# A two-layer per-position convolution: x handed over in two further layouts, the output in the residual's layout, residuals and bias loaded nearer to their use, and one half of a third of the weight tiles evicted by ScalarE

## The chip, the core and the metric

One core of one Trainium2 chip runs the program. The metric is the device time of one execution in microseconds (us). The engines are PE (TensorE, matmul), DVE (VectorE), ACT (ScalarE), POOL (GpSimd) and SP (SyncE, which here only issues DMAs).

## What is computed

Two layers of the same form, on x of shape 32 x 32 x 64 x 256 (s, b, channel, position l), float32. Each layer adds to x a convolution of width 3 along l whose weights are different at every b and l, made by a small network from z. Cut to what matters:

```python
h = relu(layernorm(z @ W1 + b1))                   # z: (b, l, 16), h: (b, l, 128)
w = (h @ W2 + b2).reshape(B, L, CI, CO, K)         # 64 x 64 x 3 weights at every (b, l)
bias = (relu(layernorm(z @ Wb1 + bb1)) @ Wb2 + bb2).transpose(0, 2, 1)
xn = groupnorm(x)                                  # mean, variance over (b, channel, 8 positions), for each s
out = einsum('sbilk,bliok->sbol', unfold(xn), w) + bias[None]
x = x + out                                        # and the same again with the second layer's weights
```

The group norm takes its mean over all b, so layer 2 cannot begin before the last of layer 1 is done.

## The kernel before, in words

**Stage 1, `first_stats` (L230).** All of x (64 MB) is read once in 16 loads of 4 MB, three buffers round, for the statistics: 512 `bn_stats` on VectorE (L278), a `merge` (L299) after every second load. Between them, in `slot` (L254), the 32 steps of the hidden network run over all engines; hidden values and bias go to DRAM (`hd`, `bd`).

**The main loop (L535 on)** has 128 chunks v = 2u + h: u counts the 32 values of b in both layers (64), h the two halves of the 64 output channels. A chunk has two phases on PE.

- *Make*: 12 tiles `pg` of 16 matmuls each (`make`, L419; L426 and L427), three PSUM buffers round. A tile holds the weights of 8 output channels at 128 pairs of positions, and is of one of three kinds. `take` (L430) evicts it, adds b2, and scatters it into the one buffer `wall` (L439). Kinds 0 and 1 take one VectorE operation over 128 partitions; kind 2 goes to two places in `wall` and takes two of 64 partitions. The order of the tiles is the list `order` (L534): the four of kind 2 first, then eight of kinds 0 and 1.
- *Products* (`products`, L445): 160 matmuls (L456; 320 records in the trace) multiply `xn` by `wall` into four tiles `pc` (two buffers). VectorE adds each into the residual `ys` (L465); in layer 1 two `bn_stats` follow (L468) for layer 2's statistics.

The products of chunk v stand behind the first make tile of chunk v+1. After them `after(v)` (L506) queues the rest: `store` (L401, four DMAs on ACT's queue), `normalize` (L412, two POOL operations, L416) for half of the s of a later u, `load_pairs` (L121) of the next input of `normalize`, `load_residual(v+3)` (L129) into the buffer that the store has just left, `add_bias(v+3)` on POOL (L399), and `load_bias(v+4)` (L386). All loads are on SP's queue. Instructions and DMA issues of one engine run in the order written; POOL runs `normalize` for one chunk behind `add_bias` of the one before, so what the add waits for holds the normalization up as well.

**Layouts.** `load_pairs` reads [s, channel, l] in runs of 1 KB and twice over (the second time shifted by one position), of which `normalize` uses every other element. `load_residual` and `store` move [s, 32 channels, 64 positions] in runs of 256 bytes, 1 MB a chunk. At the change of layer `next_stats` (L339) turns the 512 results into mean and 1/deviation; its matmuls (L367) stand in PE's queue.

Of the kernel before, what the change touches and what calls it, by code (L numbers as in the profile page):

```python
# [30 lines left out]
P = 128  # L31
# [10 lines left out]
def conv_layers(ctx: ExitStack, tc: tile.TileContext, x: bass.AP, layers: list, out: bass.AP):  # L42
    nc = tc.nc
    S, B, C, L = x.shape
# [3 lines left out]
    M = L // 2  # L48
# [9 lines left out]
    SH = S // 2  # L58
    SPLIT = 2
    NS = S // SPLIT  # L60
# [22 lines left out]
    xt = room[:, 0 : SH * L].rearrange("p (s l) -> p s l", l=L)  # L83
# [4 lines left out]
    between = const.tile([P, GT, B, NH, 6], FP, name="between")  # L88
# [29 lines left out]
    def source(u):  # L118
        return x[:, u] if u < B else x1[u - B]

    def load_pairs(u, k):  # L121
        src = source(u)[k * SH : (k + 1) * SH].rearrange("s c l -> c s l")
        nc.sync.dma_start(out=xt[0:C], in_=src)
        nc.sync.dma_start(out=xt[C:P, :, 0 : L - 1], in_=src[:, :, 1:L])

    def residual(v):
        return ys[:, v % RING]

    def load_residual(v):  # L129
        u, h = divmod(v, NH)  # L130
        for t in range(NT):
            nc.sync.dma_start(  # L132
                out=residual(v)[t * S : (t + 1) * S],
                in_=source(u)[:, h * CH : (h + 1) * CH, t * LT : (t + 1) * LT],
            )
# [94 lines left out]
    def first_stats():  # L230


        NJ = 2
        with tc.tile_pool(name="stage", bufs=1) as stage:
            spare = stage.tile([P, C // 2 * L], FP, name="spare")
            flat = [xn.rearrange("p b m s -> p (b m s)"), room, spare]
            xs = [r[:, 0 : C // 2 * L].rearrange("p (c l) -> p c l", l=L) for r in flat]
            src = x.rearrange("(q s) b (h c) l -> q (s b h) c l", s=SPLIT, h=2)
            NX = len(xs)
            for q in range(NX):  # L240
                nc.sync.dma_start(out=xs[q], in_=src[q])
                if q == 0:
                    small = [small_weights(stage, par, n) for n, par in enumerate(layers)]
            half = stage.tile([P, SPLIT, P], FP, name="half")
            nc.vector.memset(half, 0.0)
            for h in range(SPLIT):
                nc.vector.memset(half[h * C : (h + 1) * C, h, :], 1.0 / C)
# [7 lines left out]
            def slot(s, work):  # L255

                if s in made:
                    made[s].project()
                if s - 2 in made:
                    made.pop(s - 2).bias()  # L260
                if s in made:
                    made[s].root()
                for k, f in enumerate(work):
                    if k == 6 and s - 1 in made:
                        made[s - 1].scale()
                    f()
                if not work and s - 1 in made:
                    made[s - 1].scale()
                if s + 1 < U // 2:
                    made[s + 1] = Hidden(stage, zts, small, s + 1)  # L270

            parts = None
            for q in range(NS):
                if q % NJ == 0:
                    parts = stage.tile([P, NJ, G, 6], FP, tag="parts", name="parts", bufs=2)

                def piece(g, parts=parts, q=q):
                    return lambda: nc.vector.bn_stats(  # L278
                        parts[:, q % NJ, g, :], xs[q % NX][:, :, g * E : (g + 1) * E]
                    )  # L280

                for s in range(2):
                    slot(2 * q + s, [piece(g) for g in range(s * G // 2, (s + 1) * G // 2)])
                if q + NX < NS:
                    nc.sync.dma_start(out=xs[q % NX], in_=src[q + NX])
                if q + NX == NS - 1:
                    for o0 in range(0, C, 2 * OG):
                        load_w2(0, o0, o0 + 2 * OG)
                if q == NS - 3:

                    load_pairs(0, 0)
                    for v in range(RING):
                        load_residual(v)
                if q % NJ == NJ - 1:
                    merge(stage, parts, q - NJ + 1, NJ, half)
            for s in range(2 * NS, 2 * NS + 2):
                slot(s, [])

    def merge(stage, parts, q0, nj, half):  # L299
        n = nj * G  # L300
        st = parts.rearrange("p j g (two f) -> p (j g) two f", two=2)
        count = C // 2 * E
        m = stage.tile([P, n], FP, tag="mm", name="mm")
        d = stage.tile([P, n], FP, tag="md", name="md")
        v = stage.tile([P, n], FP, tag="mv", name="mv")
        nc.vector.tensor_tensor(m, st[:, :, 0, 1], st[:, :, 1, 1], ALU.add)
        nc.vector.tensor_scalar(m, m, 0.5, None, ALU.mult)
        nc.vector.tensor_tensor(d, st[:, :, 0, 1], st[:, :, 1, 1], ALU.subtract)
        nc.vector.tensor_tensor(d, d, d, ALU.mult)
        nc.vector.tensor_tensor(v, st[:, :, 0, 2], st[:, :, 1, 2], ALU.add)  # L310
        nc.vector.scalar_tensor_tensor(v, d, count / 4.0, v, ALU.mult, ALU.add)
        pm = ps_g.tile([P, SPLIT, n], FP, tag="pg", name="pm")
        for h in range(SPLIT):
            nc.tensor.matmul(pm[:, h, :], half[:, h, :], m, start=True, stop=True)
        s0 = q0 * SPLIT
        to = "p g (j h) -> p h j g"
        fr = "p h (j g) -> p h j g"
        for h in range(SPLIT):
            r = slice(h * C, (h + 1) * C)
            nc.vector.tensor_tensor(d[r], m[r], pm[r, h, :], ALU.subtract)  # L320
        nc.scalar.copy(
            gmean[:, :, s0 : s0 + nj * SPLIT].rearrange(to, h=SPLIT), pm.rearrange(fr, g=G)
        )
        nc.vector.tensor_tensor(d, d, d, ALU.mult)
        nc.vector.scalar_tensor_tensor(v, v, 1.0 / count, d, ALU.mult, ALU.add)
        pv = ps_g.tile([P, SPLIT, n], FP, tag="pg", name="pv")
        for h in range(SPLIT):
            nc.tensor.matmul(pv[:, h, :], half[:, h, :], v, start=True, stop=True)
        r = stage.tile([P, SPLIT, n], FP, tag="mr", name="mr")
        nc.scalar.activation(r, pv, AF.Sqrt, bias=eps)  # L330
        for h in range(SPLIT):
            nc.vector.reciprocal(
                rstd[:, :, s0 : s0 + nj * SPLIT].rearrange(to, h=SPLIT)[:, h],
                r.rearrange(fr, g=G)[:, h],
            )

    def next_stats(prep):

        st = between.rearrange("p g b h (two f) -> p g (b h two) f", two=2)  # L339
        n = st.shape[2]  # L340
        shape = [P, GT, n]
        m = prep.tile([P, GT], FP, name="nm")
        nc.vector.tensor_reduce(m, st[:, :, :, 1], AX.X, ALU.add)
        nc.vector.tensor_scalar(m, m, 1.0 / n, None, ALU.mult)
        v = prep.tile([P, GT], FP, name="nv")
# [3 lines left out]
        d = prep.tile([P, GT], FP, name="nd")  # L349
# [20 lines left out]
    with tc.manual_schedule():  # L370
        hs = {}
        first_stats()

        wp = ctx.enter_context(tc.tile_pool(name="wall", bufs=1))
        bp = ctx.enter_context(tc.tile_pool(name="bias", bufs=1))
        prep = ctx.enter_context(tc.tile_pool(name="prep", bufs=1))
# [24 lines left out]
        def store(v):  # L401
            u, h = divmod(v, NH)
            to = x1[u] if u < B else out[:, u - B]
            for t in range(NT):
                nc.scalar.dma_start(
                    out=to[:, h * CH : (h + 1) * CH, t * LT : (t + 1) * LT],
                    in_=residual(v)[t * S : (t + 1) * S],
                )

        def normalize(u, k):  # L410
            ss = slice(k * SH, (k + 1) * SH)
            o = xn[:, u % 2, 1 : M + 1, ss].rearrange("p (g e) s -> p s g e", g=G)  # L412
            i = xt[:, :, 0:L:2].rearrange("p s (g e) -> p s g e", g=G)
# [16 lines left out]
        def take(pg, n, kind, o0):  # L430

            if kind < 2:
                parts = [(slice(0, P), CH + (1 + kind) * CH)]
            else:
                parts = [(slice(0, C), CH + F), (slice(C, P), 0)]
            for rows, a in parts:
                nr = rows.stop - rows.start
                a += o0 % CH
                nc.vector.tensor_tensor(  # L439
                    at(wall[rows, 0, a : a + 1], [[WT, NT], [F, MT], [1, OG]]),  # L440
                    pg[rows].rearrange("p o (t m) -> p t m o", t=NT),
                    b2[n][rows, kind, None, None, o0 : o0 + OG].to_broadcast([nr, NT, MT, OG]),
                    ALU.add,
                )

# [123 lines left out]
```

## Time and profile before

| what | value |
|---|---|
| median of 3 runs | 5458.36 us (5456.52 to 5467.07) |
| the profiled execution, its own time | 5456.63 us |
| its span, first to last instruction | 5454.8 us |
| mean granted TensorE clock | 0.909 |
| busy: PE / DVE / POOL / ACT | 79% / 60% / 37% / 2% |
| moved by DMA | 784.94 MB in 1,398,552 packets, 1,098,949 of them under 512 B |

The span is divided here into stage 1 (up to about 310 us, and the first chunk up to 365 us), 64 chunks of layer 1 (to 2867 us), the change of layer, and 64 chunks of layer 2. In rows of groups, "x" is the count, the two figures behind the first bar are total busy us and mean ns of one, behind the second bar stands the idle time of the engine before them, and after "<-" what ended most of it; "issue" is idle time in which the engine waited for no semaphore. In a timeline a row has start, length, engine, line, operation, tiles, count, and in brackets the idle time before it. In rows of waits the figures are total us, times, longest. PEld is the loading of weights into PE. In rows of stretches PEclk is the granted share of the clock, and the next figure the busy share of the 16 DMA engines.

### The profile page before, as it was taken

The numbers are of one execution on the slowest core, as the hardware profiler recorded it, in microseconds if no ns is written. First come the engines' busy times: TensorE is split into PE (matmuls) and PEld (weight loads), VectorE is DVE, ScalarE is ACT, GpSimd is POOL, SyncE is SP. The second block draws the span as 40 slices with busy tenths as digits, with TensorE's granted clock in tenths as the row PEclk, the third lists the DMA queues.
The fourth block names the chain that finished last, engine by engine and source line by source line (L and its number), as shares of the span: only waits on it lengthen the run. The fifth ranks groups of instructions, "written<-read, shape, count | busy, mean of one in ns | idle before, by whom it ended". The sixth has DMA issues, their size and how long they took to land.

```text
span 5454.8 us, 191315 instructions
## 1 busy us (share of the span) xinstructions
PE 4322.6 (79%) x90760; PEld 4033.9 (74%) x90760; DVE 3269.2 (60%) x3768; ACT 118.1 (2%) x181; POOL 2034.0 (37%) x618
## 2 busy tenths in 40 slices
PE   6878788788777787887777887787777777787787
PEld 4568777777777777777767777777777777777777
DVE  7866666566566666666656555555555555565555
ACT  3410000000000000000000000000000000000000
POOL 3453433433343343334324334334334334334332
PEclk7679999999999999999989988998988998999999
DMA  8886777777777787777777778778778777778775
GB/s 308 308 171 128 141 136 132 144 130 131 135 142 130 134 148 129 133 138 143 133 143 152 137 130 130 131 132 136 133 127 136 135 130 137 134 131 144 128 133 100
DMA packets 1398552, 784.94 MB, mean 144 GB/s; under 512 B 1098949, under 2 KB 1377545, under 8 KB 1378825
## 3 DMA queue, kind: packets, MB, share of 16 engines
q1 hardware_dynamic: 829960, 616.43, 59.8%
q10 hardware_dynamic: 567808, 156.28, 15.5%
q8 instruction: 711, 11.65, 1.0%
q14 instruction: 73, 0.59, 0.0%
HBM read 625.78 MB, written 146.80 MB: 142 GB/s over the span
## 4 chain that ended last, share of the span: by engine, by line
PE 41%; POOL 17%; DVE 16%; DMA 13%; issue 10%; SPq 2%; ACT 0%; POOLq 0%; ACTq 0%; DVEq 0%
PE pc L456 23%; DVE wall L439 13%; POOL xn L416 11%; PE pg L426 10%; PE pg L427 5%; POOL room L399 5%; DMA room<-x 5%; DMA room<-in_x_dram 4%; DMA out_dram<-room 2%; SPq L132 2%; DMA x<-room 2%; PE p L175 1%; DVE room L465 1%; DVE parts L278 1%; PE p L215 1%
## 5 line engine op out<-in xcount | busy, mean ns | idle before, releaser
L426 PE MATMUL pg<-hT,w2t 128*64 128x128 f32 x24576 | 2814.8, 274 | 249.6 <-DVE wall L439 200.3
L426 PEld LDWEIGHTS pg<-hT,w2t 128*64 128x64 f32 x24576 | 2682.6, 137 | 355.3 <-PE pg L427 263.8
L427 PE MATMUL pg<-hT,w2t 128*64 128x128 f32 x24576 | 2825.5, 275 | 29.7 <-issue 29.6
L439 DVE TENSOR_TENSOR wall<-pg,b 64x1024 f32<-64x1024 f32 (+1 forms) x2048 | 2480.1, 1221 | 413.8 <-PE pg L427 369.3
L427 PEld LDWEIGHTS pg<-hT,w2t 128*64 128x64 f32 x24576 | 2682.5, 137 | 32.3 <-issue 32.1
L456 PE MATMUL pc<-wall,xn 128*32 128x128 f32 (+2 forms) x40960 | 1261.8, 289 | 761.6 <-issue 424.6
L456 PEld LDWEIGHTS pc<-wall,xn 128*32 128x32 f32 x40960 | 1188.3, 129 | 843.5 <-issue 494.4
L399 POOL TENSOR_TENSOR room<-room,bt 128x2048 f32<-128x2048 f32 x128 | 581.5, 4543 | 3124.3 <-DMA room<-x 1415.1
L465 DVE TENSOR_TENSOR room<-pc,room 128x512 f32<-128x512 f32 x512 | 354.1, 692 | 1695.2 <-PE pc L456 1619.1
L416 POOL TENSOR_TENSOR xn<-xn,rstd 128x2048 f32<-128x2048 f32 x128 | 741.0, 5789 | 10.0
L416 POOL TENSOR_TENSOR xn<-room,gmean 128x2048 f32<-128x2048 f32 x128 | 598.2, 4674 | 42.3 <-DMA room<-x 14.7
L468 DVE BATCH_NORM_STATS2 between<-room 128x6 f32<-128x256 f32 x512 | 192.9, 418 | 8.7
L187 POOL TENSOR_TENSOR sq<-sq 128x512 f32<-128x512 f32 (+2 forms) x192 | 104.3, 543 | 180.1 <-ACT sq L179 167.6
L175 PE MATMUL p<-wc,zt 17*128 17x256 f32 x256 | 108.3, 593 | 33.4 <-DMA zt<-in_L_conv_z_dram 32.6
L175 PEld LDWEIGHTS p<-wc,zt 17*128 17x128 f32 x256 | 72.5, 297 | 56.9 <-issue 39.4
L202 PEld LDWEIGHTS p<-ident,hs 128*128 128x128 f32 x256 | 49.0, 219 | 54.1 <-issue 40.2
L215 PE MATMUL p<-ht,Wb 128*64 128x512 f32 x64 | 61.6, 1065 | 10.6 <-ACT ht L205 10.6
L202 PE MATMUL p<-ident,hs 128*128 128x128 f32 x256 | 60.6, 416 | 4.6 <-DVE hs L193 4.6
L278 DVE BATCH_NORM_STATS2 parts<-xn 128x6 f32<-128x256 f32 x192 | 64.0, 407 | 0.0
L353 ACT ACTIVATE nv<-nv,eps 128x8 f32<-128x8 f32 x1 | 0.3, 300 | 2571.8 <-DVE nv L352 2571.8
L278 DVE BATCH_NORM_STATS2 parts<-room 128x6 f32<-128x256 f32 x160 | 53.4, 409 | 0.0
L278 DVE BATCH_NORM_STATS2 parts<-spare 128x6 f32<-128x256 f32 x160 | 53.4, 408 | 0.0
(61 smaller groups left out, 271.3 us busy)
## 6 DMA issues: line engine op xcount, KB each, us to landing
bt<-bd SPq DMA_DIRECT2D x512, 256.0 KB, 5.0
room<-in_x_dram SPq DMA_DIRECT2D x64, 1024.0 KB, 9.0
room<-in_x_dram SPq DMA_DIRECT2D x256, 256.0 KB, 8.5
x<-room ACTq DMA_DIRECT2D x256, 256.0 KB, 5.3
room<-x SPq DMA_DIRECT2D x64, 1024.0 KB, 9.0
room<-x SPq DMA_DIRECT2D x256, 256.0 KB, 9.5
out_dram<-room ACTq DMA_DIRECT2D x256, 256.0 KB, 5.9
room<-in_x_dram SPq DMA_DIRECT2D x64, 1020.0 KB, 14.1
```

The source lines that it names most:

```text
L175: nc.tensor.matmul(self.p1[:, k], self.zt[:, k * P : (k + 1) * P], self.t["wc"], start=True, stop=True)
L202: nc.tensor.transpose(p2[:, net, k * P : (k + 1) * P], hs[:, 2 * k + net, :], ident)
L215: nc.tensor.matmul(p3, self.t["Wb2"], self.ht[:, 1, :], start=True, stop=True)
L278: return lambda: nc.vector.bn_stats(parts[:, q % NJ, g, :], xs[q % NX][:, :, g * E : (g + 1) * E])
L399: nc.gpsimd.tensor_tensor(y, y, bts.pop(v), ALU.add)
L416: nc.gpsimd.tensor_tensor(o, i, b, op)
L426: nc.tensor.matmul(pg[0:C, k, :], w[:, k0 * C : (k0 + 1) * C], h0, start=True, stop=True)
L427: nc.tensor.matmul(pg[C:P, k, :], w[:, k1 * C : (k1 + 1) * C], h1, start=True, stop=True)
L439: nc.vector.tensor_tensor(at(wall[rows, 0, a : a + 1], [[WT, NT], [F, MT], [1, OG]]), pg[rows].rearrange("p o (t m) -> p t m o", t=NT), b2 ...
L456: nc.tensor.matmul(pc[t * S : (t + 1) * S, n0 - q * EB : n1 - q * EB, :], xn[:, u % 2, t * MT + p + 1, :], wall[:, t, a : a + (n1 - n0) * CH],
L465: nc.vector.tensor_tensor(part, pc.rearrange("p n o -> p o n"), part, ALU.add)
L468: nc.vector.bn_stats(between[:, 2 * q + g, u, h, :], part[:, :, g * E : (g + 1) * E])
```

## The change

1. The host hands x over twice: `xs` in the residual's layout (partition = position block and s; a chunk is 8 KB in a row on each partition) and `xp` in the layout of pairs (partition = parity and channel, only the elements that `normalize` uses). In layer 1 `load_pairs` is one DMA of 1 MB and `load_residual` one DMA of 1 MB, both in runs of 8 KB. `xt` then holds both halves of a u, so `load_pairs` runs a whole u ahead. Layer 2 reads x1 as before. The output is stored in the layout of `xs`, one DMA a chunk.
2. Stage 1 reads `xs`; its `bn_stats` fill the same array that layer 2 uses, and one `stats` at the end takes the place of eight `merge`. The hidden steps are spread over the 512 `bn_stats` and end with them.
3. In `after(v)`: the store is on SP's queue, ahead of the loads; `load_residual(v+2)` goes into the buffer that chunk v-1 has left; `next_pairs` (normalize and load) comes before `add_bias(v+1)`, and `load_bias(v+2)` after it.
4. In `take`, kind 2: rows 0 to 63 by VectorE as before, rows 64 to 127 by eight ScalarE activations (Identity with a bias column), one for each output channel. The order of the tiles is 2, 0, 1 four times.

```diff
+        if u < B:
+            nc.sync.dma_start(out=t, in_=xp[u, k])
+        else:
+            src = x1[u - B][k * SH : (k + 1) * SH].rearrange("s c l -> c s l")
...
+            if kind < 2:
+                add(slice(0, P), CH + (1 + kind) * CH)
+            else:
+                add(slice(0, C), CH + F)
+                rows = slice(C, P)
+                for k in range(OG):
+                    nc.scalar.activation(
+                        place(rows, 0)[:, :, :, k],
+                        pg[rows, k].rearrange("p (t m) -> p t m", t=NT),
+                        AF.Identity,
+                        bias=b2[n][rows, kind, o0 + k : o0 + k + 1],
+                    )
...
+        def after(v):
+            u, h = divmod(v, NH)
+            if v >= 0:
+                store(v)
+            if v + 2 < NH * U:
+                load_residual(v + 2)
+            if v + 1 == NH * B:
+                stats()
+                for k in range(2):
+                    next_pairs(B, k)
+            w, k = (u + 1, 1) if h == 0 else (u + 2, 0)
+            if w != B:
+                next_pairs(w, k)
+            if v + 1 < NH * U:
+                add_bias(v + 1)
+            if v + 2 < NH * U:
+                load_bias(v + 2)
...
-        order = [(2, o) for o in starts] + [(kind, o) for o in starts for kind in range(2)]
+        order = [(kind, o) for o in starts for kind in (2, 0, 1)]
```

VectorE in a chunk of layer 1, before (b_0 is the bias b2 of layer 1, 64x4x32x8 a half tile, 128x4x32x8 a whole one):

```order
L465 TENSOR_TENSOR room<-pc,room 128x32x16
L468 BN_STATS between<-room 128x6 x2
L439 TENSOR_TENSOR wall<-pg,b_0_183 64x4x32x8 x8
L439 TENSOR_TENSOR wall<-pg,b_0_183 128x4x32x8 x8
L465 TENSOR_TENSOR room<-pc,room 128x32x16
```

and after the change:

```order
L442 TENSOR_TENSOR room<-pc,room 128x32x16
L445 BN_STATS parts<-room 128x6 x2
L401 TENSOR_TENSOR wall<-pg,b_0_184 64x4x32x8
L401 TENSOR_TENSOR wall<-pg,b_0_184 128x4x32x8 x2
L401 TENSOR_TENSOR wall<-pg,b_0_184 64x4x32x8
L401 TENSOR_TENSOR wall<-pg,b_0_184 128x4x32x8 x2
```

Sixteen evictions a chunk on VectorE have become twelve, and the half tiles stand one in three.

ScalarE after the change, the last half tile of one chunk, the load of the hidden values (hT) and the first half tile of the next chunk, with the semaphores that each row waits for (before, its queue in the loop held only DMA issues):

```order
L416 ACTIVATE wall<-pg,b_1_189 64x4x32 [waits DVE_49,Activation_49]
L416 ACTIVATE wall<-pg,b_1_189 64x4x32 [waits Activation_49] x7
L116 DMA hT<-hd_124 128x256 [waits DMAHW7_49,DMAHW1_49,PE_49]
L416 ACTIVATE wall<-pg,b_1_189 64x4x32 [waits DVE_49,PE_49,Activation_49]
L416 ACTIVATE wall<-pg,b_1_189 64x4x32 [waits Activation_49] x7
```

The first activation of a tile waits for a count of VectorE that stands for VectorE's half of the same tile; the first of a chunk waits for the products too, since they read `wall`. The counts of ScalarE itself are those of the chunk before.

SP's queue for one chunk of layer 2, before (x_12, x_13 are x1 of two values of b, L123 and L124 pairs, L132 residuals, L392 bias):

```order
L123 DMA room<-x_12_84 64x16x256
L124 DMA room<-x_12_84 64x16x255
L132 DMA room<-x_12_84 32x32x64 x4
L392 DMA bt<-bd_158 32x2048 x4
L123 DMA room<-x_13_85 64x16x256
```

and after (L372 is the store, L143 the residuals, L131 and L132 the pairs, L354 the bias):

```order
L372 DMA out_dram<-room 128x2048
L143 DMA room<-x_12_84 32x32x64 x4
L131 DMA room<-x_13_85 64x16x256
L132 DMA room<-x_13_85 64x16x255
L354 DMA bt<-bd_158 32x2048 x4
```

The store has come into SP's queue, one DMA in place of four on ACT's, and the residuals stand ahead of the pairs.

More of the change, by code (lines that the diff above doesn't have):

```diff
@@ L57, in conv_layers @@
     U = NL * B
[L58 to L60 removed]
+    SV = 4
     BLK = 2 * L
@@ L87, in conv_layers @@
     rstd = const.tile([P, G, S], FP, name="rstd")
-    between = const.tile([P, GT, B, NH, 6], FP, name="between")
+    parts = const.tile([P, GT, B, NH, 6], FP, name="parts")
+    prep = const.tile([P, 3, GT], FP, name="prep")
     ident = const.tile([P, P], FP, name="ident")
@@ L272, in first_stats @@
[L272 to L335, printed above, removed]
@@ L337, in next_stats, with step @@
-    def next_stats(prep):
-        st = between.rearrange("p g b h (two f) -> p g (b h two) f", two=2)
+            def step(s, half):
+                if half == 0:
+                    if s in made:
+                        made[s].project()
+                    if s - 2 in made:
+                        made.pop(s - 2).bias()
+                    if s in made:
+                        made[s].root()
+                else:
+                    if s - 1 in made:
+                        made[s - 1].scale()
+                    if s + 1 < U // 2:
+                        made[s + 1] = Hidden(stage, zts, small, s + 1)
```

198 lines of the change are left out of this document (106 added, 92 removed).

## The prediction, made before the changed kernel was run

> **What bounds the kernel now.** Read first are the spans of the page, its queues, and a row each from the rows of waits.
>
> ```profile
> span 5454.8 us, 191315 instructions
> PE 4322.6 (79%) x90760; PEld 4033.9 (74%) x90760; DVE 3269.2 (60%) x3768; ACT 118.1 (2%) x181; POOL 2034.0 (37%) x618
> q8 instruction: 711, 11.65, 1.0%
> q10 hardware_dynamic: 567808, 156.28, 15.5%
> POOL room L399 <- DMA room<-x: 1415.1, 58, 38.9
> PE pc L456 <- issue: 424.6, 204, 6.2
> PE pc L456 <- POOL xn L416: 335.2, 62, 8.2
> PE pg L426 <- DVE wall L439: 200.3, 406, 0.6
> ```
>
> PE is the engine to follow. It idles for three reasons, all in the main loop. For 424.6 us it waits for no semaphore in the products. For 335.2 us the products wait for POOL's normalization, which stands on POOL behind an add that waits for residuals (1415.1 us). For 200.3 us a make tile waits until VectorE has emptied a buffer.
>
> Next is the timeline of VectorE: the last products of a chunk (L465), from chunk to chunk.
>
> ```profile
> 365.43 0.69 DVE L465 TENSOR_TENSOR room<-pc,room 128x512 f32<-128x512 f32 x1 [0.58 <-PE pc L456]
> 1704.70 0.69 DVE L465 TENSOR_TENSOR room<-pc,room 128x512 f32<-128x512 f32 x1 [1.70 <-PE pc L456]
> 1706.10 13.42 DVE L439 TENSOR_TENSOR wall<-pg,b 64x1024 f32<-64x1024 f32 x11
> 1719.91 1.23 DVE L439 TENSOR_TENSOR wall<-pg,b 128x1024 f32<-128x1024 f32 x1 [0.38 <-PE pg L427]
> 1721.65 1.23 DVE L439 TENSOR_TENSOR wall<-pg,b 128x1024 f32<-128x1024 f32 x1 [0.52 <-PE pg L427]
> 1739.79 0.69 DVE L465 TENSOR_TENSOR room<-pc,room 128x512 f32<-128x512 f32 x1 [0.92 <-PE pc L456]
> 1782.93 0.69 DVE L465 TENSOR_TENSOR room<-pc,room 128x512 f32<-128x512 f32 x1 [1.92 <-PE pc L456]
> 2866.67 0.69 DVE L465 TENSOR_TENSOR room<-pc,room 128x512 f32<-128x512 f32 x1 [1.74 <-PE pc L456]
> 2926.37 0.69 DVE L465 TENSOR_TENSOR room<-pc,room 128x512 f32<-128x512 f32 x1 [1.66 <-PE pc L456]
> 5444.50 0.69 DVE L465 TENSOR_TENSOR room<-pc,room 128x512 f32<-128x512 f32 x1 [2.11 <-PE pc L456]
> ```
>
> A chunk takes (2866.67 - 365.43) / 63 = 39.70 us in layer 1, (5444.50 - 2926.37) / 63 = 39.97 in layer 2; the start is 365.4, the change of layer 59.7, the tail 10.3. Chunks alternate: 35.1 (1704.70 to 1739.79), then 43.1 (to 1782.93). In the make phase eleven half-tile evictions run back to back for 13.42 us, so VectorE sets its first half. Later tiles come every 1.745 us (1719.91 to 1721.65) with VectorE idle in between: there PE sets the pace.
>
> The third view is of stretches, for the product matmuls alone: a disturbed chunk (three rows), a quiet one in layer 1, a quiet one in layer 2.
>
> ```profile
> 1690.60:1694.70 4.10, 4.04 (x176) 3.82 (x168) 1.00 1.18 189
> 1694.70:1697.80 3.10, 0.00 (x0) 0.00 (x0) 0.94 1.38 161
> 1697.80:1701.00 3.20, 0.15 (x9) 0.15 (x12) 0.50 0.96 140
> 1731.00:1739.70 8.70, 8.02 (x320) 7.46 (x320) 1.00 0.02 5
> 4480.50:4491.90 11.40, 8.23 (x320) 7.47 (x320) 1.00 0.47 72
> 2950.00:5400.00 2450.00, 1943.71 (x42930) 1865.04 (x42918) 1345.76 (x1220) 0.00 (x0) 904.55 (x183) 0.92 0.78 133
> ```
>
> All 320 matmul records take 8.70 us when the DMA engines are quiet (0.02), 11.40 when half busy. In the disturbed chunk PE stands for over 3 us under full DMA load, and afterwards the granted clock is 0.50. I read these stalls as waits for PE's own instructions: q8 brought 711 blocks of 16 KB, and PE's 2 x 90,760 instructions make 709 blocks of 256. Such a fetch queues with the other DMA traffic.
>
> A sentence beside these rows: the Trainium skill ("Runtime: NRT & Kernel Launch", "Instruction fetch mechanics") says that instructions are refilled in blocks of 16 KiB while the engine executes, and that this is hidden. The size agrees (11.65 MB / 711 blocks); that it is hidden does not (424.6 us).
>
> **The change, part by part.**
>
> *Normalization before the add, residuals into a buffer long free.* The products' wait of 335.2 us goes: SP issues store, residuals and pairs in turn, and nothing on POOL ahead of the normalization waits for the residuals of the chunk just stored. The work is as before:
>
> ```profile
> L416 POOL TENSOR_TENSOR xn<-room,gmean 128x2048 f32<-128x2048 f32 x128 | 598.2, 4674 | 42.3 <-DMA room<-x 14.7 <-DMA room<-in_x_dram 13.9 <-ACT gmean L368 13.7
> L416 POOL TENSOR_TENSOR xn<-xn,rstd 128x2048 f32<-128x2048 f32 x128 | 741.0, 5789 | 10.0
> L399 POOL TENSOR_TENSOR room<-room,bt 128x2048 f32<-128x2048 f32 x128 | 581.5, 4543 | 3124.3 <-DMA room<-x 1415.1 <-DMA room<-in_x_dram 1200.3 <-DVE wall L439 411.7
> room<-x SPq DMA_DIRECT2D x64, 1020.0 KB, 13.4
> ```
>
> POOL needs 4.67 + 5.79 + 4.54 = 15.0 us a chunk. Residuals and pairs (each up to about 13.4) land within 27 us of the store, and the bias behind them; all results are due a chunk later: nothing here is late in a chunk of over 30 us.
>
> *DMA.* Layer 1's loads become runs of 8 KB, so the products run in quiet queues: I take the quiet row, 8.7. Layer 2 keeps its loads; the store alone shrinks, from q10's 15.5% of 5454.8 us over 128 chunks (6.6 us a chunk) to about 3.4 (13.5 us for 4 MB in the row below, a quarter). Its DMA work is then 0.78 x 39.97 - 6.6 + 3.4 = 28.0 us a chunk, under a chunk of 33: not the bound, but queues stay busy during products. I take 11.5 from the row of 11.40.
>
> *Make.* Twelve tiles at PE's pace take 12 x 1.745 = 20.9 us. VectorE has 12 operations of 1.22 (14.6 us), spread one in three, so its queue no longer limits. ScalarE's eight activations now stand behind VectorE's half of the same tile, and the PSUM buffer is free when both are done. Nothing of before has this operation (64 x 128, PSUM to scattered SBUF); behind it on ScalarE's queue stands only the load of hidden values, once in two chunks and due a chunk later. The nearest rows:
>
> ```profile
> L439 DVE TENSOR_TENSOR wall<-pg,b 64x1024 f32<-64x1024 f32 x1024 | 1249.9, 1221 | 48.7 <-DMA room<-in_x_dram 17.2 <-PE pg L427 8.2
> L330 ACT ACTIVATE mr<-pv,eps 128x128 f32<-128x128 f32 x8 | 2.9, 367 | 2.0 <-PE pv L328 1.9
> L217 ACT ACTIVATE bs<-p,bb 64x512 f32<-64x512 f32 x32 | 23.1, 722 | 29.8 <-PE p L215 29.8
> 246.77 0.76 ACT L205 ACTIVATE ht<-p,be,g 128x512 f32<-128x512 f32 x1
> 247.43 0.77 ACT L205 ACTIVATE ht<-p,beb,gb 128x512 f32<-128x512 f32 x1
> ```
>
> One activation of 128 elements from PSUM with a bias takes 0.367. Of two in a row the second starts 0.10 before the first ends, so each further one costs 0.27: 7 x 0.27 + 0.367 = 2.26 for eight. A tile is free 1.22 + 2.26 + 0.1 for two semaphores = 3.6 us after its make; two further makes cover 3.49, so a trio waits 0.1. After products VectorE first ends its L465 and L468: in the rows above the matmuls end at 1739.70 and its first eviction starts at 1741.18 (1706.10 after 1704.70 likewise), 1.5 us late; the first half tile is then free at 1.5 + 1.22 + 2.26 + 0.07 = 5.05, against 3.49: a wait of 1.56 once a chunk (0.9 in layer 2, without L468). With 0.3 for the other three waits the make phase takes 20.94 + 1.56 + 0.3 = 22.8 us, in layer 2 22.1. From 0.27 the bounds go up to 0.722 an activation, the row of four times as many elements; down, nothing is gained below the 20.9 of PE.
>
> Beside the row of 0.367: the Trainium skill ("ScalarE: Activation LUTs", "What ACT_TABLE_LOAD costs") gives about 280 ns + 0.833 ns an element with a pointer as bias, and an overlap of 93 ns back to back; by it, as an estimate, an activation takes 387 ns, eight 2.45 us, the make phase about 0.75 us more and the kernel about 4590 us. The same page ("Rules for kernel authors") tells to add on VectorE, not ScalarE, which speaks against this split; VectorE's 13.42 us back to back speak for it.
>
> *Start.* Statistics, the loads for them, and the step from sums to normalization as the change of layer shows it:
>
> ```profile
> 26.07 7.20 DVE L278 BATCH_NORM_STATS2 parts<-xn 128x6 f32<-128x256 f32 x22
> L193 DVE TENSOR_TENSOR hs<-p,var 128x1024 f32<-128x1024 f32 x32 | 39.2, 1225 | 2.8
> L191 DVE RECIPROCAL var<-var 128x8 f32<-128x8 f32 x32 | 6.1, 190 | 13.0 <-ACT var L188 12.8
> xn<-in_x_dram SPq DMA_DIRECT2D x6, 4096.0 KB, 13.5
> 2870.54 1.51 DVE L343 TENSOR_REDUCE nm<-between 128x8 f32<-128x1024 f32 x1
> 2885.09 4.66 POOL L416 TENSOR_TENSOR xn<-room,gmean 128x2048 f32<-128x2048 f32 x1 [13.72 <-ACT gmean L368]
> ```
>
> Statistics begin at 26.07 and run at 7.20 / 22 = 0.327 us each: 26 + 512 x 0.327 + 39.2 + 6.1, and the 13.0 that VectorE waits in the hidden network, make 252. (The loads, 16 x 13.5 = 216 us, stay ahead.) `stats` takes 14.6 (2870.54 to 2885.09, where normalization starts), two normalizations 2 x 10.5: products could start at 288. Their weights need the last hidden values by way of DRAM; I allow 20 for that, and 22.8 of make end near 297. Between 288 and 297 I take the later; with 8.7 of products chunk 0 ends at **306**, before 365.4.
>
> *Change of layer and tail.* POOL now has three normalizations with two loads of 13.4 between them ahead of `add_bias`. The first starts 18.4 after the last L465 (2866.67 to 2885.09); 3 x 10.5 of normalization and, for two loads of 13.4, what of them no normalization covers (some 16) put the add's end, 4.54 later, at about 70. The first L465 needs it and the other three follow: the next chunk ends at **75**, now 59.7. The tail: one store of 1 MB at 3.4 plus its start, **6** for 10.3.
>
> *Sum.* 306 + 63 x (22.8 + 8.7) + 75 + 63 x (22.1 + 11.5) + 6 = 306 + 1984.5 + 75 + 2116.8 + 6 = 4488 of span. The profiled execution took 5456.63, 1.8 above its span and 1.7 below the median of 5458.36; with 1.8 the forecast is **4490 us**.
>
> **Rivals.** *No overlap of the activations* (0.22). After VectorE's half-tile operations nothing overlaps in these rows (13.42 for eleven is 11 x 1.22), and partitions and targets differ from the L205 pair. Eight then take some 3.04 (0.38 each), 0.78 more; four trios a chunk, the make phase is 25.9 and 25.2: 63 x 6.2 = 390, about **4880**.
>
> *Products of layer 2 stay in traffic* (0.13). Store, residuals and pairs are issued at the end of products, in one row on SP, so fetches could meet the load that 1694.70 to 1697.80 shows, with half clock behind. At 16 for 11.5 this costs 63 x 4.5 = 284: **4775**. Against it: SP's bursts start after the products and 28.0 us of work fits between two of them.
>
> *Fetches hidden in both layers* (0.05): products at the matmul pace (176 records in 4.10 us, 320 in 7.45), 63 x (1.25 + 4.05) = 334 less: **4160**. That is what the Trainium skill's section on instruction fetch would have; the quiet row, at 8.70, speaks against.
>
> *Slower* (0.04): scattered writes of single elements, `F` apart in `wall`, cost ScalarE more than its other targets. At 0.722 an activation eight take 5.8, 3.5 more a trio, 14 a chunk: 126 x 14 = 1764, about **6250**. It decides where the 968 us that I forecast are used up: 968 / 126 / 4 = 1.9 a trio, eight activations 2.26 + 1.9 = 4.2, so 0.52 each. For it stands only that no row shows such a write by ScalarE; against it, that VectorE's scatter of 1024 takes 1.22, no more than L193's 1.225 into rows.
>
> **How the numbers follow.** The forecast has 0.56, the rivals 0.22, 0.13, 0.05 and 0.04. The forecast's own bounds, 30 us at start and change of layer, 1 us a chunk in the products (126) and 0.2 a chunk in the make phase, give 4310 to 4670. The range of **4290 to 4950** reaches over the first two rivals with their own spread and leaves out the other two and the first two at once. About 0.2% (11 us) is what a measurement can tell from no change; all cases but the last lie far below: faster **0.95**, same **0.01**, slower **0.04**.
>
> **What would show it right or wrong.** Right: the products no longer wait for POOL's normalization; VectorE's evictions mostly wait for PE; an activation repeats every 0.27 us; products take 8.7 in layer 1; DMA share in layer 2 is near 28.0 / 33.6 = 0.83; chunk 0 ends near 306. Wrong: a make tile that waits for ScalarE for more than 0.5 us in every trio, products in layer 2 with stalls of 3 us and half clock, a first eviction of a chunk held by something other than L465 and L468, or an add that the products wait for.

## The result, and the profile after

The changed kernel takes 4602.90 us (median of 4 runs, 4594.60 to 4614.89) against 5457.44 before: a ratio of 0.8434, 95% interval 0.8412 to 0.8457. The forecast was 4490, range 4290 to 4950. The profiled execution took 4594.60, its span is 4592.5.

The page after, the head, the fetch queue and PE's groups; then, from the rows of waits, all of PE's that belong to the main loop and exceed 5 us:

```profile
span 4592.5 us, 193878 instructions
PE 4069.4 (89%) x90704; PEld 3883.6 (85%) x90704; DVE 2642.2 (58%) x3168; ACT 1291.2 (28%) x4264; POOL 2074.9 (45%) x618
DMA packets 760621, 718.23 MB, mean 156 GB/s; under 512 B 567492, under 2 KB 715016, under 8 KB 716296
q8 instruction: 709, 11.62, 1.1%
L391 PE MATMUL pg<-hT,w2t 128*64 128x128 f32 x24576 | 2808.4, 278 | 60.7 <-issue 60.6
L390 PE MATMUL pg<-hT,w2t 128*64 128x128 f32 x24576 | 2808.6, 278 | 56.5 <-issue 48.2
L433 PE MATMUL pc<-wall,xn 128*32 128x128 f32 (+2 forms) x40960 | 1047.4, 261 | 313.3 <-issue 288.9
```

```profile
PE pc L433 <- issue: 288.9, 157, 6.3
PE pg L391 <- issue: 60.6, 24, 4.5
PE pg L390 <- issue: 48.2, 18, 4.6
PE pc L433 <- DVE room L442: 16.8, 1, 16.8
PE pg L390 <- DVE wall L401: 5.5, 29, 0.2
PE pc L433 <- POOL xn L380: 5.1, 1, 5.1
```

The 862 us come off PE's row: 253 fewer busy us (4322.6 to 4069.4; the mean granted clock rose from 0.909 to 0.944), 448 less idle time before the products' matmuls (761.6 to 313.3) and 162 less before the makes (249.6 + 29.7 to 56.5 + 60.7); together 863. The products' wait for POOL fell from 335.2 to 5.1, the makes' wait for VectorE from 200.3 to 5.5. Of the idle time that is left in these rows, 397.7 us carry no semaphore.

The last L442 of the first and last chunk of each layer, on VectorE's timeline:

```profile
327.48 0.69 DVE L442 TENSOR_TENSOR room<-pc,room 128x512 f32<-128x512 f32 x1 [0.29 <-PE pc L433]
2326.68 0.69 DVE L442 TENSOR_TENSOR room<-pc,room 128x512 f32<-128x512 f32 x1 [2.56 <-PE pc L433]
2399.74 0.69 DVE L442 TENSOR_TENSOR room<-pc,room 128x512 f32<-128x512 f32 x1 [1.80 <-PE pc L433]
4587.06 0.69 DVE L442 TENSOR_TENSOR room<-pc,room 128x512 f32<-128x512 f32 x1 [2.43 <-PE pc L433]
```

Start 327.5 (forecast 306), a chunk of layer 1 31.73 (31.5), change of layer 73.1 (75), a chunk of layer 2 34.72 (33.6), tail 5.4 (6). In PE's records of the trace, the products of layer 1 alternate between 8.0 and 11.9 us on average, and the makes of layer 2 between 21.2 and 26.6. Why every second chunk? Four stretches of layer 2 (products, make, products, make):

```profile
3643.40:3659.70 16.30, 9.38 (x324) 8.61 (x322) 2.08 (x3) 0.00 (x0) 8.29 (x2) 0.90 0.61 131
3659.70:3680.80 21.10, 21.10 (x389) 20.93 (x385) 15.26 (x13) 9.04 (x32) 6.93 (x2) 1.00 0.24 71
3680.80:3689.60 8.80, 7.61 (x324) 7.36 (x324) 2.08 (x3) 0.00 (x0) 0.00 (x0) 1.00 0.84 169
3689.60:3717.50 27.90, 23.99 (x389) 23.58 (x388) 15.26 (x13) 9.06 (x32) 15.30 (x3) 0.88 1.06 233
```

The last three figures of a row are granted clock, DMA share and GB/s. The makes run without a gap while the DMA engines have little to do (0.24), and stretch to 27.9 us at a share of 1.06. The DMA issues of SP and ScalarE in the same 60 us show who bunches the loads:

```profile
3660.53 0.36 SPq L372 DMA_DIRECT2D out_dram<-room  x1
3660.93 22.91 SPq L143 DMA_DIRECT2D room<-x  x4
3683.95 1.06 SPq L131 DMA_DIRECT2D room<-x  x1
...
3690.46 0.37 SPq L372 DMA_DIRECT2D out_dram<-room  x1
3690.87 15.67 SPq L143 DMA_DIRECT2D room<-x  x4
```

```profile
3676.99 2.26 ACT L416 ACTIVATE wall<-pg,b 64x128 f32<-64x128 f32 x8 [2.98 <-DVE wall L401]
3679.17 0.33 ACTq L116 DMA_DIRECT2D hT<-hd  x1
```

SP needs 22.91 us for four residual loads that take 0.3 to 0.7 each to issue. Its waits name the cause, in layer 2 (L143) and in layer 1 (L140):

```profile
SPq L143 <- DMA hT<-hd: 595.0, 29, 22.4
SPq L140 <- DMA hT<-hd: 481.7, 28, 18.0
```

In this program the completion semaphores of these DMAs are eight (DMAHW0 to 7), dealt out in turn to the DMAs of both queues, SP's and ScalarE's; a DMA is issued only when the one before it on the same semaphore has landed. Every second chunk the turn of a residual load falls to the semaphore of `hT`, which ScalarE issues only when the makes that read the old hidden values are through. SP stands, pairs and bias behind it, and then the loads of two chunks run in one.

### The profile page after: what moved, and what is told of

It reads as the page before. It is cut to its first block, busy times and chain, and to the rows that moved or that the text cites. A ratio compares the mean times of both kernels' runs of the same rounds, so it can differ in the third digit from the quotient of the medians.

```text
span 4592.5 us, 193878 instructions
## 1 busy us (share of the span) xinstructions
PE 4069.4 (89%) x90704; PEld 3883.6 (85%) x90704; DVE 2642.2 (58%) x3168; ACT 1291.2 (28%) x4264; POOL 2074.9 (45%) x618
## 3 DMA queue, kind: packets, MB, share of 16 engines
q1 hardware_dynamic: 724488, 683.80, 56.5%
## 4 chain that ended last, share of the span: by engine, by line
PE 82%; issue 9%; DVE 3%; DMA 3%; POOL 2%; ACT 1%; ACTq 0%; SPq 0%; POOLq 0%; DVEq 0%
PE pg L390 48%; PE pc L433 23%; PE pg L391 10%; DVE wall L401 2%; POOL sq L198 1%; DMA bd<-bs 1%; PE p L186 1%; DMA zt<-in_L_conv_z_dram 1%; DVE parts L445 1%; DVE room L442 1%; DMA room<-x 1%; PE p L226 0%; ACT ht L216 0%; ACT sq L190 0%; PE p L213 0%
## 5 line engine op out<-in xcount | busy, mean ns | idle before, releaser
L391 PE MATMUL pg<-hT,w2t 128*64 128x128 f32 x24576 | 2808.4, 278 | 60.7 <-issue 60.6
L390 PE MATMUL pg<-hT,w2t 128*64 128x128 f32 x24576 | 2808.6, 278 | 56.5 <-issue 48.2
L390 PEld LDWEIGHTS pg<-hT,w2t 128*64 128x64 f32 x24576 | 2758.8, 140 | 82.3 <-issue 61.9
L391 PEld LDWEIGHTS pg<-hT,w2t 128*64 128x64 f32 x24576 | 2759.2, 140 | 60.7 <-issue 60.7
L401 DVE TENSOR_TENSOR wall<-pg,b 128x1024 f32<-128x1024 f32 (+1 forms) x1536 | 1869.0, 1220 | 870.7 <-PE pg L391 866.8
L416 ACT ACTIVATE wall<-pg,b 64x128 f32<-64x128 f32 x4096 | 1176.7, 481 | 3090.3 <-DVE wall L401 2224.6
L433 PE MATMUL pc<-wall,xn 128*32 128x128 f32 (+2 forms) x40960 | 1047.4, 261 | 313.3 <-issue 288.9
L433 PEld LDWEIGHTS pc<-wall,xn 128*32 128x32 f32 x40960 | 988.9, 114 | 379.1 <-issue 351.9
L442 DVE TENSOR_TENSOR room<-pc,room 128x512 f32<-128x512 f32 x512 | 354.1, 692 | 1002.4 <-PE pc L433 883.7
L380 POOL TENSOR_TENSOR xn<-xn,rstd 128x2048 f32<-128x2048 f32 x128 | 782.5, 6113 | 10.0
L361 POOL TENSOR_TENSOR room<-room,bt 128x2048 f32<-128x2048 f32 x128 | 593.4, 4636 | 82.3 <-DMA bt<-bd 72.3
L445 DVE BATCH_NORM_STATS2 parts<-room 128x6 f32<-128x256 f32 x512 | 192.9, 418 | 8.7
L287 DVE BATCH_NORM_STATS2 parts<-room 128x6 f32<-128x256 f32 x160 | 53.5, 412 | 0.0
```

Source lines behind the costliest of these rows:

```text
L287: nc.vector.bn_stats(parts[:, g, u, h, :], xv[q % NX][:, j, :, g * E : (g + 1) * E])
L361: nc.gpsimd.tensor_tensor(y, y, bts.pop(v), ALU.add)
L380: nc.gpsimd.tensor_tensor(o, i, b, op)
L390: nc.tensor.matmul(pg[0:C, k, :], w[:, k0 * C : (k0 + 1) * C], h0, start=True, stop=True)
L391: nc.tensor.matmul(pg[C:P, k, :], w[:, k1 * C : (k1 + 1) * C], h1, start=True, stop=True)
L401: nc.vector.tensor_tensor(place(rows, a), pg[rows].rearrange("p o (t m) -> p t m o", t=NT), b2[n][rows, kind, None, None, o0 : o0 + OG].to ...
```

## The experiments

Each run stands against runs of the kernel before on the same chip. The table gives the median and the ratio to before, with its interval.

| run | what | us | ratio |
|---|---|---|---|
| the change | | 4602.9 | 0.8434 (0.8412 to 0.8457) |
| e1 | without ScalarE's half | 4584.3 | 0.8374 (0.8351 to 0.8397) |
| e2 | old order of tiles | 4715.0 | 0.8622 (0.8601 to 0.8643) |
| e4 | residuals three ahead | 4631.6 | 0.8480 (0.8460 to 0.8501) |
| e13 | parts 1 and 2 alone | 4750.6 | 0.8704 (0.8687 to 0.8721) |
| e6 | part 3 alone | 5542.1 | 1.0128 (1.0109 to 1.0147) |
| e10 | part 3 alone, `hT` last on SP | 5646.7 | 1.0343 (1.0313 to 1.0373) |
| e12 | part 3 alone, `hT` first on SP | 5228.2 | 0.9573 (0.9558 to 0.9588) |
| e5 | part 4 alone | 5451.6 | 0.9969 (0.9956 to 0.9982) |
| e7 | the change, `hT` last on SP | 4469.8 | 0.8180 (0.8159 to 0.8201) |
| e11 | the change, `hT` first on SP | 4310.6 | 0.7890 (0.7875 to 0.7905) |
| e8 | the change, runs of 8 KB in layer 2 | 4252.6 | 0.7787 (0.7771 to 0.7802) |
| e14 | e1, e11 and two more edits | 4314.7 | 0.7896 (0.7879 to 0.7912) |

**ScalarE or the order of the tiles?** e1 undoes the activations, e2 the order:

```diff
-                for k in range(OG):
-                    nc.scalar.activation(
...
+                add(slice(C, P), 0)
```

> The changed kernel, but VectorE evicts both halves of the third kind, in the new order of tiles. Theory 'the order is what frees VectorE': a trio costs VectorE 4 x 1.22 = 4.9 us against PE's 5.24, so only the first tile after products is late (1.5 + 2 x 1.22 = 3.94 against 3.49, 0.5 us a chunk in layer 1, none in layer 2): about 4630 us. Rival 'ScalarE's share is needed': the make phase goes back to its 24.0 and 23.3 us of before, +2.3 a chunk: about 4880 us.

```diff
-        order = [(kind, o) for o in starts for kind in (2, 0, 1)]
+        order = [(2, o) for o in starts] + [(kind, o) for o in starts for kind in range(2)]
```

> The changed kernel, but the four tiles of the third kind stand first again, ScalarE keeping its half. Theory 'the order is what counts': four half tiles in a row put four times 2.26 us on ScalarE against PE's 1.745, PE is 3.1 us late by the seventh tile, so the make phase is some 24.0 us in layer 1 and 23.5 in layer 2: about 4870 us. Rival 'the relief of VectorE is what counts, whatever the order': within 50 us of the changed kernel's 4603.

e1 came out at 4584, not above the change but below it (the intervals do not touch). VectorE's timeline in e1, one trio as one row (two half tiles and two whole ones):

```profile
1706.94 4.85 DVE L401 TENSOR_TENSOR wall<-pg,b 64x1024 f32<-64x1024 f32 x4 [0.52 <-PE pg L391]
1712.17 4.84 DVE L401 TENSOR_TENSOR wall<-pg,b 64x1024 f32<-64x1024 f32 x4 [0.39 <-PE pg L391]
```

VectorE alone needs 4.85 us for a trio that takes PE 3 x 1.745 = 5.24, and then waits 0.39 for PE. ScalarE's half is not needed. e2 lost 112 us, in the direction of the first theory but less than half of what it had; with ScalarE in the old order PE does wait for it:

```profile
PE pg L390 <- ACT wall L416: 91.7, 106, 3.8
```

The order carries this part of the gain, and with the old one ScalarE is the late engine.

**Which part took away the wait for POOL?** e6 puts the third part alone on the kernel before, e4 undoes its distances in the changed kernel, e13 has only the layouts and the first stage (store on ScalarE's queue, old order, no activations, three ahead):

```diff
+            if v + 2 < NH * U:
+                load_residual(v + 2)
             if v + 1 == NH * B:
...
-            if v + RING < NH * U:
-                load_residual(v + RING)
-                add_bias(v + RING)
-            if v + RING + 1 < NH * U:
-                load_bias(v + RING + 1)
+            if v + 1 < NH * U:
+                add_bias(v + 1)
+            if v + 2 < NH * U:
+                load_bias(v + 2)
```

> The kernel before with the third part of the change alone (store on SP, residuals two ahead, normalization before the bias, bias one ahead), old layouts, old evictions. Theory 'the late normalization is the larger loss': the products' 335 us of waiting for POOL go, and with them half clock behind stalls: 4900 to 5120 us. Rival 'it is the traffic of short runs': the wait for POOL turns into stalls with no semaphore, 5300 us or more.

e4 and e13 carry the same lines the other way round.

> The changed kernel, with residuals and the add three chunks ahead and the bias four, as before, loads into the buffer just stored, behind the pairs on SP. Theory 'the distance is what keeps the normalization on time': the add waits on POOL for loads again, and the products for POOL, 335 us or a good part: 4750 to 4950 us. Rival 'the layouts do it, the distance nothing': 4570 to 4650 us.

> The first two parts of the change alone: new layouts and the first stage, with residuals three ahead, stores on ScalarE's queue, all evictions on VectorE and the old order of tiles. Theory 'layouts and order of tiles add up, the rest counts little': 4632 us with residuals three ahead, and 2.3 us a chunk for the old order with VectorE alone (24.0 and 23.3 for 21.6 and 21.2): 4880 to 4960 us. Rival 'layouts need the third part in layer 2, where runs are as short as before': its products wait for POOL as before, 5050 us or more.

The third part alone is 1.3% slower than before. That lies in the rival's range, but neither theory fits: the wait for POOL does go (23.6 us), and most of what comes in its place is a wait with a semaphore. SP's, VectorE's and PE's waits in e6:

```profile
SPq L392 <- DMA hT<-hd: 1991.1, 59, 46.8
DVE room L465 <- POOL room L399: 742.4, 93, 38.4
PE pc L456 <- DVE room L465: 410.7, 80, 17.2
PE pc L456 <- POOL xn L416: 23.6, 2, 15.3
```

Here it is the bias loads that draw the semaphore of `hT`; they stand up to 46.8 us, and with the bias only one chunk ahead the add is late, VectorE waits for it, and the next products wait for VectorE. e4 stayed at 4632 (0.5% over the change): the distance counts little once the layouts are there. e13, the layouts alone, reached 4751. Its PE rows:

```profile
PE pc L426 <- issue: 297.6, 149, 6.3
PE pg L390 <- DVE wall L401: 181.7, 368, 0.6
PE pc L426 <- POOL xn L380: 10.3, 7, 4.7
```

With residuals three ahead and adds behind loads, as before, the 335.2 us of waiting for POOL are 10.3. So either part takes the wait away by itself: the layouts in e13, the third part in e6. Only the layouts bring the time with it. How they do it is plain in layer 1, where POOL's adds wait less for their loads (540.3 us from 400 to 2300, 976.7 before). In layer 2 the loads are as before and only the store has a new layout: from 2960 to 4700 the adds wait for loads almost as long (901.0 us, 1009.0 before), and yet the products wait 5.7 us for POOL, where it was 133.3. What went there is SP's standing for the store ahead of the residual loads (494.9 us before, none in e13); that this is the cause was not tested. The makes still wait 181.7 for VectorE. e13 was faster than both of my bounds.

**Part 4 alone.** e5 is the kernel before with the lines of e1 and e2 the other way round.

> The kernel before with the fourth part of the change alone (ScalarE's half and the new order of tiles). Theory 'POOL and its loads set the length of a pair of chunks': a shorter make phase is given back as a longer wait of the products for POOL, at most the quiet chunk gains 2.3 us: 5310 to 5450 us. Rival 'make and products add up': every chunk gains 2.2 to 2.4 us, about 5170 us.

It took 5452, 2 us above the first theory's range, but its rows do not bear that theory out: the wait for POOL fell to 126.0 us, and a new one stands in the makes:

```profile
PE pg L426 <- DVE wall L437: 343.1, 296, 1.3
PE pc L469 <- issue: 552.4, 197, 6.7
PE pc L469 <- POOL xn L416: 126.0, 54, 11.9
```

Some two make tiles a chunk wait for the eviction of the tile just before them. Why they get that buffer stays open. e5 only shows that part 4 brings 0.3% by itself.

**The load of the hidden values.** e7 and e10 move `hT` to the end of `after(v)` on SP, in the changed kernel and in e6; e11 and e12 ahead of the store:

```diff
         def after(v):
             u, h = divmod(v, NH)
+            if h == 0 and u + 1 < U:
+                hs[u + 1] = load_hidden(u + 1)
             if v >= 0:
                 store(v)
...
-            if h == 0 and u + 1 < U:
-                hs[u + 1] = load_hidden(u + 1)
```

> The changed kernel; the load of the hidden values, which alone stays on ScalarE's queue, goes to the end of SP's work for a chunk, half a chunk ahead of its use. In the changed kernel SP's residual load stands behind that load's semaphore every second chunk (1077 us in all, up to 22 each), and the loads of two chunks fall into one. Theory 'this lumping costs': SP no longer stands, both chunks of a pair become alike, and a third or more of the excess of the heavy chunk (2.1 us a chunk in layer 1, 5 in layer 2) goes: 4350 to 4500 us. Rival 'the stalls go with the bytes, lumped or spread': 4570 to 4630 us.

> The kernel before with the third part of the change alone, which by itself took 5542 us, and the load of the hidden values on SP's queue as in the run beside it. Theory 'the third part alone lost because SP's bias loads stand behind the semaphore of that load (1991 us)': they no longer stand, the add is on time, and the 335 us of the products' wait for POOL go after all: 4950 to 5200 us. Rival 'with the old layouts the traffic takes it all': 5400 us or more.

> As the run with the hidden values on SP's queue (4470 us), but this load stands ahead of the store of a chunk, not behind its loads; there it landed late, and make tiles waited 219 us for it. Theory 'those 219 us are all that is wrong with it': 4220 to 4270 us. Rival 'they cover another wait at the same place (an instruction fetch in the burst of loads)': 4400 us or more.

> The kernel before with the third part of the change alone, and the load of the hidden values on SP's queue ahead of the store. The run with that load at the end took 5647 us, but its make tiles waited 719 us for it, so it told nothing. Theory 'rid of that load, the third part brings the 335 us of the products' wait and the half clock behind it': products of some 14 and 8 us, 4850 to 5000 us. Rival 'old layouts leave no room for loads, whatever their order': 5300 us or more.

e7 gained 3% (4470), inside the first theory's range, although it brought a wait of its own: the load came behind 4 MB of others and the makes waited for it. The row of e7, and that of e10, in which the same wait hid all else:

```profile
PE pg L390 <- DMA hT<-hd: 219.0, 38, 7.6
```

```profile
PE pg L426 <- DMA hT<-hd: 718.8, 64, 20.2
```

e11 is rid of it: 4311, 6% under the change, at a granted clock of 0.973 for 0.944. That is 40 us above the first theory's range. Its PE rows:

```profile
PE pc L433 <- issue: 202.0, 221, 2.7
PE pg L390 <- issue: 7.2, 15, 1.6
PE pg L391 <- issue: 6.0, 15, 0.6
```

Stalls come more often in the products (221 for 157) but end after 2.7 us, where they lasted up to 6.3; in the makes they are nearly gone. e12 says what the third part is worth once `hT` does not couple the queues: 4.3%, less than I expected, with the wait for POOL gone (11.2 us) and stalls without a semaphore in its place:

```profile
PE pc L456 <- issue: 588.6, 213, 6.2
```

**What the stalls are.** e8 gives layer 2 as many bytes in long runs, by reading x in the layouts of layer 1 in place of x1:

```diff
-            src = x1[u - B][k * SH : (k + 1) * SH].rearrange("s c l -> c s l")
-            nc.sync.dma_start(out=t[0:C], in_=src)
...
+            for j in range(2):
+                nc.sync.dma_start(
+                    out=xt[:, j * SH * M : (j + 1) * SH * M], in_=xp[u - B, j].rearrange("p s m -> p (s m)")
+                )
...
+            nc.sync.dma_start(out=residual(v), in_=xs[:, v - NH * B])
```

> The changed kernel, but layer 2 reads x, in the layouts of layer 1, in place of x1: as many bytes for pairs and residuals, in runs of 8 KB instead of 1 KB and 256 bytes. Layer 2 so computes from other data. Theory 'the stalls without a semaphore are instruction fetches behind many short packets': a chunk of layer 2 falls from 34.7 us to layer 1's 31.7 or below: 4350 to 4450 us. Rival 'bytes count, not runs': 4570 to 4630 us.

It fell by 350 us, further than the theory had it. Layer 2 as one stretch, in the change, in e11 and in e8:

```profile
2420.00:4580.00 2160.00, 1887.03 (x43711) 1839.29 (x43710) 1075.27 (x993) 563.22 (x1984) 924.12 (x182) 0.95 0.66 151
```

```profile
2360.00:4290.00 1930.00, 1773.76 (x42520) 1725.68 (x42514) 1050.32 (x969) 551.37 (x1941) 903.37 (x178) 0.99 0.75 166
```

```profile
2420.00:4230.00 1810.00, 1776.41 (x43516) 1743.93 (x43514) 1070.17 (x988) 565.75 (x1969) 931.59 (x182) 1.00 0.55 180
```

Against the change, e8 moves more GB/s (180 for 151) at a smaller DMA share (0.55 for 0.66) and a full clock: as many bytes, in the whole run in 388,908 packets for 760,621. But e8 changes one thing more in layer 2. With one DMA for the residuals in place of four the turn of the semaphores falls otherwise, and SP no longer stands for `hT` there: 595.0 us in the change, no such row in layer 2 of e8 (in layer 1 the wait stays, 482.8). So e8 is to be held against e11, where SP does not stand either. By VectorE's timeline a chunk of layer 2 takes 34.72 us in the change, 31.92 in e11 and 29.31 in e8: by e11, about half of e8's gain in layer 2 is the coupling; the other half comes with the long runs (e8's loads are also fewer, and its `hT` stays on ScalarE's queue). PE's stalls in the products, in the stretches above, first e11, then e8:

```profile
PE pc L433 <- issue: 144.3, 128, 2.7
```

```profile
PE pc L430 <- issue: 26.0, 50, 1.1
```

These are 321 MB in 395,094 packets in e11 and 327 MB in 51,117 in e8. So with the coupling gone in both it is the short packets, or the DMA time that they take (a share of 0.75 for 0.55), and not the bytes, that PE stands behind. That it stands for its own instructions is shown by where it stands: in the changed kernel's records the stalls from 3645 to 3790 us are 256 PE instructions apart, or multiples of it, within the few records that are missing, and q8 brings a block for each 256.

**A version from all this.** e14 takes e1 and e11, puts the first add of layer 2 ahead of its normalizations, and stores x1 a second time in the residual's layout:

```diff
+                nc.sync.dma_start(out=xr[v], in_=residual(v))
...
+            nc.sync.dma_start(out=residual(v), in_=xr[v - NH * B])
...
             if v + 1 == NH * B:
+                add_bias(v + 1)
+                load_bias(v + 2)
                 stats()
```

> A version from what was found: the changed kernel with all evictions on VectorE (4584 us by itself), the load of the hidden values ahead of the store on SP, the first add of layer 2 ahead of its normalizations (27 us of waiting at the change of layer), and x1 stored a second time in the residual's layout, so that layer 2's residuals come in runs of 8 KB. Theory 'short runs cost, an extra store in long runs is cheap': 4080 to 4200 us. Rival 'the extra store costs layer 1 what layer 2 gains': 4200 to 4260 us.

It missed both: three runs took 4304 to 4316, the same as e11. Its profiled execution took 13,420 us, with a mean of 669 ns in the records of the makes' matmuls for 278 in the change, and tells nothing of the others, so there is no profile to say which of the edits gave back what another brought. That stays open. e11 and e14 are the fastest of the versions that read the reference's data.

## Why the prediction was right, and where it was wrong

The time lay in the range, 2.5% over the forecast, and faster was right. Of its sum, 4488 against a span of 4592.5, the terms missed by +21.5 (start), +14.7 (63 chunks of layer 1), -1.9 (change of layer), +70.5 (63 chunks of layer 2) and -0.6 (tail).

*Make.* "Eight take 2.26" was right to the digit (2.26 in the rows of ScalarE above): the activations overlap, although base and target differ from the pair that the estimate came from, and so the first rival fell, and with it the scattered write of the last one. The Trainium skill's figure ("ScalarE: Activation LUTs", "What ACT_TABLE_LOAD costs") made 2.45 of it; the measurement decides. The kernel stands near the 4590 worked out from that page for other reasons. The waits of 1.56 and 0.3 a chunk did not come (5.5 us in the whole run): the program gives the fourth tile the buffer of the second, which VectorE alone empties, and the first tile's, which waits for ScalarE, goes to the fifth. So quiet makes took 21.6 and 21.2 for 22.8 and 22.1. But "VectorE's 13.42 us back to back speak for" the split did not hold: the order alone cures them, and the Trainium skill's rule to add on VectorE ("ScalarE: Activation LUTs", "Rules for kernel authors") is the better advice here, by the 0.7% that e1 shows.

*"The products' wait of 335.2 us goes"* was right, and the cause named was one of two. I gave it to the third part, which does take the wait away (23.6 us in e6, 11.2 in e12); but so do the layouts alone (10.3 in e13), and the time hangs on them: e13 gains 13%, where the third part alone lost 1.3%, and 4.3% are gained once `hT` is out of its way. The row that says that POOL's add waits 1415.1 us for `room<-x`, from which I read a place in a queue, does not tell what holds the products up: in e13 it still has 1173.8.

*"Nothing here is late in a chunk of over 30 us"* is the step that failed. I named what stands behind the activations on ScalarE, "only the load of hidden values, once in two chunks and due a chunk later", and found nobody who waits for it. SP does, through a shared semaphore, for 1077 us. From that come the makes of 26.6 us in layer 2, for which I had 22.1, and the products of 11.9 in layer 1, for which I had 8.7. The shorter products of the quiet chunk (8.0, and 8.5 in layer 2 for 11.5) give much of it back in the sum, so that the total hides two errors of opposite sign. e11 undoes the coupling: its products take 8.6 on average in layer 1, close to the forecast of 8.7, which was their cost without it.

*Products of layer 2.* They took 8.5 and 13.5 in turn, 11.0 on average for 11.5, so their mean was right, though not from one quiet row. The second rival (stalls of 3 us and half clock in the products of layer 2) came true in part, and in the makes too: 108.8 us of make idle time are without a semaphore. The third (fetches hidden) did not: 397.7 us of stalls stayed. The DMA share in layer 2, forecast as 0.83, was 0.66: some 23 us of DMA work a chunk (0.66 x 34.72) for 28.0. The section of the Trainium skill ("Runtime: NRT & Kernel Launch", "Instruction fetch mechanics") agrees in the size of a block and not in that it is hidden.

*Start.* 21.5 us late. The recorded sum is also 2 us off in itself: its terms for the weights, as far as they are given (252 + 20 + 22.8), make 295 and not 297. I took VectorE's waits for ScalarE's roots as before, 13.0 us; the row after has 38.0, since statistics and hidden network now end together and nothing else fills the gap:

```profile
L202 DVE RECIPROCAL var<-var 128x8 f32<-128x8 f32 x32 | 6.5, 202 | 38.0 <-ACT var L199 37.3
```

*Change of layer* (73.1 for 75) and *tail* were right, by the mechanism named: VectorE waits 27 us for POOL's add behind three normalizations.

## What to carry to other kernels

The same wait can be taken away by moving a transfer or by shortening it. Shorten first (long runs): here either one ended the products' wait for POOL, but only the long runs gained 13%, and they also take work off whatever shares the DMA engines, the instruction fetch of a busy engine included. Before a transfer is moved, look in the waits of every queue for one that stands behind a DMA of another queue: completion semaphores dealt out in turn couple queues that share no data. And undo each part of a change by itself: here two parts together were worth 13%, one 0.3% alone, one was a loss alone, and the fix of a side effect 6%. An experiment can undo more than it is meant to: e8 also broke the coupling, which only the waits of SP's queue show.

## What the runs showed of the hardware that was not expected

- Eight activations of 64 x 128 from PSUM with a bias column take 2.26 us in a row, single elements scattered in the target.
- PE's instruction fetch is slowed by short packets, not by bytes: with the coupling gone in both, the products of layer 2 stalled for 26.0 us at 180 GB/s in long runs (e8), for 144.3 at 166 GB/s in short ones (e11).
- Many short stalls cost less clock than fewer long ones: e11 has 221 stalls in the products, 202.0 us in all, with 2.7 us as the longest, and a clock of 0.973; e8 has 117, only 151.0 us in all, but with up to 6.0, and a clock of 0.960.
